# A score matrix product by seven products, split into two passes with a second level of seven

## The chip, the cores and the metric

The kernel runs on one core of one Trainium2 chip. The metric is the device time of one execution in microseconds. A core has a matrix engine (PE, with its weight loads shown apart as PEld), a vector engine (DVE), a scalar engine (ACT), a further elementwise engine (POOL) and a queue engine that here issues the DMAs (SP). Matrix products are summed in PSUM, which has eight banks of 128 x 512 fp32; everything else lies in SBUF or in DRAM.

## The reference, cut to what matters

One layer of a perceiver: cross-attention of 128 latents `x` to a context of 12544 rows, then a small linear attention and a feed-forward block on the 128 latents.

```
q = (layernorm(x) @ Wq) per head / sqrt(128)      # 16 heads, 128 queries
k = ctx @ Wk ; v = ctx @ Wv                       # ctx: 12544 x 512
attn = softmax(q k^T) ; x = x + (attn v) @ Wo
x = x + linear_attention(layernorm(x)) ; x = x + ffn(layernorm(x))
```

Nearly all the work lies in the first attention. The kernel folds `Wk` into the queries: `kq = Wk_h q_h^T` for all heads is a 512 x 2048 matrix (16 heads x 128 queries), so the scores are `ctx (12544 x 512) @ kq (512 x 2048)`. The weighted sums are then `ctx^T @ exp(scores)`, and `Wv`, `Wo` are applied to the small result.

## The kernel before

**Stages in order.** A prologue makes `kq` (lines L356 and L385). The scores stage (L196) makes all scores and stores them in DRAM (`sc`). The weighing stage (L490) reads them back, subtracts the column maximum, takes the exponential, and multiplies with the context. The rest of the layer works on 128 rows.

**fp32 as three products.** An operand is cut in a high part (a rounded copy, type fp32r, by ACT) and a low part (operand minus high part, by DVE). A product is three matrix products, low x high, high x low and high x high, summed in one PSUM bank.

**The scores stage.** The context has 49 row pairs `i` (two blocks of 128 rows), the columns of `kq` two halves `f` of 1024. A unit `(i, f)` is a 256 x 512 by 512 x 1024 product, done by the Strassen-Winograd scheme: seven products of 128 x 256 by 256 x 512 instead of eight. The context's sums are `S1..S4` (`sum_ct`, DVE, L169 to L172), the column sums `T1..T4` are made once. A product is two contraction chunks of three matmuls, so six matmuls; a unit is 42, and the stage 98 x 42 = 4116. Out of the products come four blocks of the scores:

```
p1 = A11 B11   p6 = S2 T2   p7 = S3 T3   p5 = S1 T1   p4 = A22 T4   p2 = A12 B21   p3 = S4 B22
u2 = p1 + p6   u3 = u2 + p7
c11 = p1 + p2   c22 = u3 + p5   c21 = u3 + p4   c12 = u2 + p5 + p3
```

DVE adds (L225) read one product from PSUM and one sum from SBUF; ACT copies `p1` and `c11` out (L231, L260); DVE keeps a running maximum (L243); one 1 MB store for each unit goes to DRAM (L235). PSUM holds eight banks in turn.

**What sets the order.** The steps stand on each engine in the order in which they are written (`seq`); in the prologue and the first four units this order is written out by hand as a list of names (`plan`), after that a scheduler of the framework places them. The pairs go `(i, 0), (i, 1)` for i from 2; at the end both last pairs of half 0 go before those of half 1, so that POOL can reduce the maximum of half 0 over the partitions (L592) while PE still works on half 1, and the first exponentials are ready when the scores end (`beside`).

**The weighing stage.** 98 steps of 128 rows for each half; a step is 24 matmuls (two column halves, four blocks of the context, three parts), with DVE and ACT preparing the exponentials two steps ahead (`soften`, `high_part`, `low_part`, `total`).

Of the kernel before, what the change touches and what calls it, by code (L numbers as in the profile page):

```python
# [16 lines left out]
P = 128  # L17
D = 512
# [15 lines left out]
def tile_perceiver_layer(  # L34
# [34 lines left out]
    x1 = const.tile([P, D], F32, name="x1")  # L69
# [62 lines left out]
    S1, S2, S3, S4, A11, A12, A22, A21 = range(8)  # L132
    B11, T2, T3, T1, T4, B21, B22 = range(7)
# [4 lines left out]
    ctp = att.enter_context(tc.tile_pool(name="ct", bufs=2))  # L138
    mxp = att.enter_context(tc.tile_pool(name="mx", bufs=1))
    p1x = ExitStack()  # L140
    tmp = p1x.enter_context(tc.tile_pool(name="tmp", bufs=1))
    kqx = ExitStack()
    kq1p = ctx.enter_context(tc.tile_pool(name="kq1", bufs=1, side="right"))
    kq0p = kqx.enter_context(tc.tile_pool(name="kq0", bufs=1, side="right"))
    kq = {}

    def right(f, s, n):

        if (f, s) not in kq:
            kq[f, s] = (kq0p, kq1p)[f].tile([P, 2, 2, 512], F32R, name=f"kq{f}_{s}")  # L150
        return kq[f, s][:, n, :, :]

    def spare(s, shape):

        return kq1p.tile(shape, F32, name=f"kq1_{s}")

    def load_ct(i):
        if i == 1:
            raw = spare(B22, [P, 8, 2, P])
        else:  # L160
            raw = ctp.tile([P, 8, 2, P], F32, tag="raw", name="ctr", bufs=1)
        nc.sync.dma_start(out=raw[:, A11:, :, :], in_=cT[i])
        return raw

    def sum_ct(raw):

        r = lambda s: raw[:, s, :, :]
        return [
            lambda: nc.vector.tensor_tensor(r(S1), r(A21), r(A22), ALU.add),  # L169
            lambda: nc.vector.tensor_tensor(r(S3), r(A11), r(A21), ALU.subtract),  # L170
            lambda: nc.vector.tensor_tensor(r(S2), r(S1), r(A11), ALU.subtract),
            lambda: seq(nc.vector.tensor_tensor(r(S4), r(A12), r(S2), ALU.subtract)),  # L172
        ]

    def high_ct(raw):
        hi = ctp.tile([P, 7, 2, P], F32R, tag="hi", name="cth")
        return hi, nc.scalar.copy(hi, raw[:, :7, :, :])  # L177

    def low_ct(raw, hi, lo=None):
        if lo is None:  # L180
            lo = ctp.tile([P, 7, 2, P], F32R, tag="lo", name="ctl")
        return lo, nc.vector.tensor_tensor(lo, raw[:, :7, :, :], hi, ALU.subtract)  # L182

    cts, raws, mx = {}, {}, {}

    def unit(i, f, place):

        t = {}

        def product(ps, a, b, first):  # L190
            n = 0
            hi, lo = cts[i]
            for cc in range(2):
                for lt, part in ((lo, 0), (hi, 1), (hi, 0)):
                    place(
                        nc.tensor.matmul(  # L196
                            ps, lhsT=lt[:, a, cc, :], rhs=right(f, b, part)[:, cc, :], start=(first and n == 0),
                            stop=(n == 5), skip_group_check=True,
                        )
                    )  # L200
                    n += 1

        def fresh(p, a, b):
            def emit():
                t[p] = ps_s.tile([P, 512], F32, tag="s", name="ps")
                product(t[p], a, b, True)

            return emit

        def onto(p, a, b):  # L210
            return lambda: product(t[p], a, b, False)

        def out(j, b):
            if "so" not in t:
                t["so"] = iop.tile([P, 2, 1024], F32, tag="io", name="so")
            return t["so"][:, j, b * 512 : (b + 1) * 512]

        def add(name, p, q):
            def emit():
                if name in ("u2", "u3"):  # L220
                    t[name] = tmp.tile([P, 512], F32, tag=name, name=name)
                    to = t[name]
                else:
                    to = out(*name)
                place(nc.vector.tensor_tensor(to, t[p], t[q], ALU.add))  # L225

            return emit

        def p1s():
            t["p1s"] = tmp.tile([P, 512], F32, tag="p1", name="p1s")  # L230
            place(nc.scalar.copy(t["p1s"], t["p1"]))  # L231

        def c12():
            add((0, 1), "p5", "u2")()
            nc.sync.dma_start(out=sc_d[i][f], in_=t["so"])  # L235

        def larger(j):
            def emit():
                if f not in mx:
                    mx[f] = mxp.tile([P, 1024], F32, name=f"mx{f}")  # L240
                    place(nc.vector.tensor_tensor(mx[f], t["so"][:, 1, :], t["so"][:, 0, :], ALU.max))
                elif i > 0:
                    place(nc.vector.tensor_tensor(mx[f], mx[f], t["so"][:, j, :], ALU.max))  # L243

            return emit

        return t, {
            "p1": fresh("p1", A11, B11),
            "p1s": p1s,
            "p6": fresh("p6", S2, T2),  # L250
            "U2": add("u2", "p6", "p1s"),
            "p7": fresh("p7", S3, T3),
# [11 lines left out]
        }  # L264

# [64 lines left out]
    for h2 in range(4, 8):  # L335
        ws.append(load_w(h2))
        begin(*ws[h2][2])
        if h2 == 4:
            raws[1] = load_ct(1)
# [1187 lines left out]
```

## Time and profile before

| | us |
|---|---|
| three timed runs | 2111.97, 2112.01, 2112.11; median 2112.01 |
| span of the profiled execution, first to last instruction | 2109.8 |
| median less the span (what lies around it) | 2.2 |

The profile gives the span of its execution; no other time of that execution is listed. It was taken on the one core at a granted PE clock of 1.000.

| part of the span | from, us | length, us |
|---|---|---|
| prologue, up to the first scores matmul | 0 | 35.55 |
| scores, 4116 matmuls | 35.55 | 933.19 |
| weighing, 4704 matmuls | 968.75 | 1066.24 |
| the rest of the layer | 2034.98 | 74.8 |

The busy columns of a page say how long an engine had an instruction running; the line after a bar in a group says how long the engine stood idle before these instructions and whom it waited for.

### The profile page before, as it was taken

What the parts mean: (1) busy time and instruction counts of PE and PEld (TensorE: products, weight loads), DVE (VectorE), ACT (ScalarE), POOL (GpSimd) and SP (SyncE); (2) the same over time, 40 slices, a digit from 0 to 9 for tenths busy, and PEclk for the clock granted to TensorE, in tenths of its full rate; (3) what the DMA queues carried; (4) which work ended last, traced back from release to release, by engine and by line L of the source; (5) the groups of instructions that cost most, each with busy time, mean ns of one, the idle gap of its engine ahead of it and who ended that gap; (6) DMA issues with size and microseconds to landing.
All of it is one profiled execution on the core that took longest, in us unless ns stands there. A gap on an engine that the chain in (4) does not pass through costs nothing.

```text
span 2109.8 us, 24119 instructions
## 1 busy us (share of the span) xinstructions
PE 2103.4 (100%) x9614; PEld 1742.1 (83%) x9614; DVE 1689.0 (80%) x1908; ACT 776.9 (37%) x898; POOL 55.6 (3%) x23
## 2 busy tenths in 40 slices
PE   9999999999999999999999999999999999999999
PEld 8888888888888888888888888888888888888896
DVE  6877777777777777778897888879898887777767
ACT  6222122221222122214444444445544455444445
POOL 0000000000000000000000000003020000000010
PEclk9999999999999999999999999999999999999999
DMA  6333333333333333336564455555545454434443
GB/s 216 142 137 138 132 150 130 141 129 150 130 150 128 142 143 137 140 150 229 200 237 152 172 207 199 200 199 185 184 155 195 157 202 161 141 143 145 150 156 126
DMA packets 73877, 341.74 MB, mean 162 GB/s; under 512 B 8451, under 2 KB 12803, under 8 KB 46499
## 3 DMA queue, kind: packets, MB, share of 16 engines
q1 hardware_dynamic: 73622, 340.09, 43.7%
q8 instruction: 75, 1.23, 0.2%
q14 instruction: 36, 0.29, 0.0%
q10 hardware_dynamic: 144, 0.13, 0.0%
HBM read 228.76 MB, written 111.43 MB: 161 GB/s over the span
## 4 chain that ended last, share of the span: by engine, by line
PE 99%; DVE 1%; ACT 0%; DMA 0%; issue 0%; DVEq 0%
PE pu L490 51%; PE ps L196 44%; PE pq L356 1%; PE pk L385 1%; PE pc L897 1%; PE po L932 1%; PE py L1438 0%; PE pv L1112 0%; DMA x<-in_x_dram 0%; DVE uT L1408 0%; PE pq L1112 0%; PE pk L1112 0%; PE pp L1249 0%; DVE am L1425 0%; DVE st L1381 0%; PE ph L1352 0%
## 5 line engine op out<-in xcount | busy, mean ns | idle before, releaser
L196 PE MATMUL ps<-kq,cth 128*128 128x512 f32 x2744 | 844.9, 389 | 0.0
L490 PE MATMUL pu<-ph,cl 128*128 128x512 f32 x1568 | 610.0, 389 | 0.0
L490 PE MATMUL pu<-pl,ch 128*128 128x512 f32 x1568 | 610.0, 389 | 0.0
L490 PE MATMUL pu<-ph,ch 128*128 128x512 f32 x1568 | 610.0, 389 | 0.0
L196 PEld LDWEIGHTS ps<-kq,cth 128*128 128x128 f32 x2744 | 515.0, 188 | 107.0
L196 PE MATMUL ps<-kq,ctl 128*128 128x512 f32 x1344 | 522.8, 389 | 0.0
L544 ACT CAST ph<-si 128x1024 fp32r<-128x1024 f32 x194 | 204.1, 1052 | 449.5 <-PE pu L490 449.1
L490 PEld LDWEIGHTS pu<-ph,ch 128*128 128x128 f32 x1568 | 294.3, 188 | 61.2
L490 PEld LDWEIGHTS pu<-ph,cl 128*128 128x128 f32 x1568 | 294.3, 188 | 61.1
L490 PEld LDWEIGHTS pu<-pl,ch 128*128 128x128 f32 x1568 | 294.3, 188 | 61.0
L225 DVE TENSOR_TENSOR so<-ps,u 128x512 f32<-128x512 f32 x294 | 202.6, 690 | 133.9 <-PE ps L196 129.5
L196 PEld LDWEIGHTS ps<-kq,ctl 128*128 128x128 f32 x1344 | 252.3, 188 | 52.3
L260 ACT COPY so<-ps 128x512 f32<-128x512 f32 x98 | 57.7, 589 | 577.4 <-PE ps L196 577.4
L532 DVE TENSOR_TENSOR cl<-cr,ch 128x1024 fp32r<-128x1024 f32 x98 | 126.2, 1288 | 167.5 <-ACT ch L526 167.5
L539 ACT ACTIVATE si<-si 128x1024 f32<-128x1024 f32 x194 | 205.5, 1059 | 96.6 <-DVE si L538 96.6
L549 DVE TENSOR_TENSOR pl<-si,ph 128x1024 fp32r<-128x1024 f32 x194 | 240.0, 1237 | 1.0 <-ACT ph L544 1.0
L243 DVE TENSOR_TENSOR mx<-mx,so 128x1024 f32<-128x1024 f32 x190 | 232.1, 1222 | 6.8
L538 DVE TENSOR_TENSOR si<-si,mb 128x1024 f32<-128x1024 f32 x194 | 235.4, 1214 | 0.0
L557 DVE TENSOR_TENSOR lsum<-lsum,si 128x1024 f32<-128x1024 f32 x192 | 233.7, 1217 | 0.0
L526 ACT CAST ch<-cr 128x1024 fp32r<-128x1024 f32 x98 | 102.4, 1045 | 0.1
L177 ACT CAST cth<-ctr 128x1792 fp32r<-128x1792 f32 x48 | 81.8, 1703 | 37.8 <-PE ps L196 35.4
L182 DVE TENSOR_TENSOR ctl<-ctr,cth 128x1792 fp32r<-128x1792 f32 x47 | 94.9, 2019 | 0.7 <-ACT cth L177 0.7
(291 smaller groups left out, 872.7 us busy)
## 6 DMA issues: line engine op xcount, KB each, us to landing
sc<-so SPq DMA_DIRECT2D x98, 1024.0 KB, 3.8
si<-sc SPq DMA_DIRECT2D x97, 1024.0 KB, 5.1
cr<-in_c_dram SPq DMA_DIRECT2D x98, 512.0 KB, 3.5
ctr<-in_cT_dram SPq DMA_DIRECT2D x48, 512.0 KB, 3.5
kq<-in_w1T_dram SPq DMA_DIRECT2D x16, 512.0 KB, 4.2
kq<-in_w2T_dram SPq DMA_DIRECT2D x16, 512.0 KB, 4.0
ternary<-kq SPq DMA_DIRECT2D x4, 1024.0 KB, 10.2
kq<-ternary SPq DMA_DIRECT2D x4, 1024.0 KB, 9.4
```

Of the source, the lines that this page charges most:

```text
L182: return lo, nc.vector.tensor_tensor(lo, raw[:, :7, :, :], hi, ALU.subtract)
L196: nc.tensor.matmul(ps, lhsT=lt[:, a, cc, :], rhs=right(f, b, part)[:, cc, :], start=(first and n == 0), stop=(n == 5), skip_group_check=True,)
L225: place(nc.vector.tensor_tensor(to, t[p], t[q], ALU.add))
L243: place(nc.vector.tensor_tensor(mx[f], mx[f], t["so"][:, j, :], ALU.max))
L490: nc.tensor.matmul(pu[b][cc], lhsT=lt[:, j, cs], rhs=rt[:, bs], start=(first and n == 0), stop=(last and n == 2))
L526: seq(nc.scalar.copy(ctx_hi[f, i], ctx_raw[f, i]))
L532: seq(nc.vector.tensor_tensor(ctx_lo[f, i], ctx_raw[f, i], ctx_hi[f, i], ALU.subtract))
L538: seq(nc.vector.tensor_tensor(exps[k], exps[k], mb[f], ALU.subtract))
L539: seq(nc.scalar.activation(exps[k], exps[k], AF.Exp))
L544: seq(nc.scalar.copy(high[k], exps[k]))
L549: seq(nc.vector.tensor_tensor(low[k], exps[k], high[k], ALU.subtract))
L557: seq(nc.vector.tensor_tensor(lsum[f], lsum[f], exps[k], ALU.add))
```

## The change

The scores stage is written anew; prologue, weighing stage and the rest keep their work.

**Groups and slots.** Two row pairs are taken together, times both halves: 24 groups of four units (`"00"`, `"01"`, `"10"`, `"11"`: pair, half), and pair 48 alone. A slot is the three matmuls of one contraction chunk of 128. A product of one unit is two slots, so four units need eight slots for it.

**A second level of seven.** For `p1`, `p6` and `p7` the four units of a group form again a 2 x 2 by 2 x 2 block product (pairs x chunks by chunks x halves). The function `wide` makes them with seven slots, from sums of the left blocks (`left_sums`, now on POOL) and of the `kq` blocks (`sums`, made once). The other four products stay eight slots (`direct`).

**Two passes.** The first pass goes over all groups with 22 slots each: `p1` (7), `p2` (8) and `p6` (7); it stores `c11` and, for later, `u2`. The second goes over all groups with 31 slots: `p7` (7), `p5`, `p3`, `p4` (8 each); it loads `u2` and stores `c22`, `c12`, `c21`. The `kq` operands of the second pass are put into DRAM early in the first (`put_by`) and brought back (`bring_back`).

**Seeded banks.** A sum that was an elementwise add is now made in PSUM: ACT copies the earlier sum from SBUF into a bank (`act(ps, ...)`), and the matmuls are added onto it (`start=False`). Inside `wide` the bank is read ("tapped") between two slots while later slots go on adding to it.

**Order.** All steps up to the first exponentials are given to a planner (`Plan`) with an engine, a length, what they read and write, and a due time. It walks through time, gives each engine that is free the ready step with the earliest due time, and the order that comes out is the program's. It counts for `n` elements 0.09 + 0.00097 n us on ACT, 0.157 + 0.00104 n on DVE, 0.2 + 0.0021 n on POOL, and 0.68 us a slot; it lets no POOL step run beside a DVE step marked `port` (both inputs in SBUF).

**Smaller parts.** Every score block has a store of its own (262 KB in place of 1 MB), the context's blocks are loaded in pieces of 262 KB, some of them twice. The last pair comes first in the first pass and last in the second; the maximum of half 0 is complete only with its `c21`. The first exponentials' loads and steps are given to the planner too.

Core of the diff (the new functions that the text speaks of; the removed ones are those named above):

```diff
+    W_LEFT = ("a00", "a01", "s2", "s3", "a11", "s1", "s4")
+    W_SLOTS = (("p1", 0), ("p6", 5), ("p2", 6), ("p7", 10), ("p5", 11), ("p4", 15), ("p3", 16))
+    def wide(R_, h, x, z, y, t0, dst, fold=None):
...
+        def tap(u, n):
+            if fold:
+                dve(dst[u], x, fold[u], ALU.add, after(n), port=False)
+            else:
+                act(dst[u], x, after(n))
+        slot(x, a["a00"], R_["b00"], True, due["p1"])
+        if fold:
+            dve(z, x, fold["00"], ALU.add, after("p1"), port=False)
+        else:
+            act(z, x, after("p1"))
+        slot(x, a["s2"], R_["t2"], False, due["p6"])
+        tap("01", "p6")
+        slot(z, a["a01"], R_["b10"], False, due["p2"])
+        act(dst["00"], z, after("p2"))
+        slot(x, a["s3"], R_["t3"], False, due["p7"])
+        tap("11", "p7")
+        slot(y, a["s1"], R_["t1"], True, due["p5"])
+        dve(dst["11"], y, dst["11"], ALU.add, after("p5"), port=False)
+        slot(x, a["a11"], R_["t4"], False, due["p4"])
+        tap("10", "p4")
+        slot(y, a["s4"], R_["b11"], False, due["p3"])
+        dve(dst["01"], y, dst["01"], ALU.add, after("p3"), port=False)
+    def left_sums(a, due):
+        s = lambda k: left_raw(a + k)
+        pool(s(2), s(0), s(1), ALU.add, due)
+        pool(s(6), s(2), s(4), ALU.subtract, due)
+        pool(s(7), s(4), s(0), ALU.subtract, due)
+        pool(s(3), s(5), s(6), ALU.subtract, due)
...
+    def first(g):
+        n, G = g % 2, TA + 22 * SLOT * g
+        wide(R[1], 0, bank(0), bank(2), bank(3), G, m1s)
+        for u, s0, s1 in D_FIRST:
...
+            act(ps, m1s[u], G + (s0 - 1.5) * SLOT)
+            direct(ps, D_HI[n], D_LO[n], R[2], r_, f, G + s0 * SLOT, G + s1 * SLOT, False)
+            act(c11, ps, G + (s1 + 1) * SLOT)
+            largest(ps, f, 0, G + (s1 + 1.5) * SLOT, True)
+            store(c11, pair_of(g, u), f, 0, 0, G + (s1 + 2) * SLOT)
+        u2 = dict(zip(UNIT, u2c))
+        wide(R[6], 14, bank(1), bank(2), bank(4), G + 14 * SLOT, u2, m1s)
...
+    def second(g):
+        G = TB + 31 * SLOT * g
...
+        u2 = {u: load_u2(g, u, G - 14 * SLOT) for u in at_slots}
+        wide(R[7], 0, bank(0), bank(2), bank(3), G, m7s)
+        for u, (a0, a1, b0, b1, c0_, c1) in at_slots.items():
...
+            act(ps, u2[u], t(a0 - 2))
+            direct(ps, *S1_, R[5], r_, f, t(a0), t(a1), False)
+            dve(c22, ps, m7s[u], ALU.add, t(a1 + 1), port=False)
+            pool(u2[u], u2[u], m7s[u], ALU.add, t(a1 + 1))
+            largest(c22, f, 1, t(a1 + 3), False)
+            store(c22, i, f, 1, 1, t(a1 + 3))
+            direct(ps, *S4_, R[3], r_, f, t(b0), t(b1), False)
+            act(c12, ps, t(b1 + 1))
+            largest(ps, f, 1, t(b1 + 1.5), True)
+            store(c12, i, f, 0, 1, t(b1 + 2))
...
+            act(ps4, u2[u], t(c0_ - 2))
+            direct(ps4, *A22_, R[4], r_, f, t(c0_), t(c1), False)
+            act(c21, ps4, t(c1 + 1))
+            largest(ps4, f, 0, t(c1 + 1.5), True)
+            store(c21, i, f, 1, 0, t(c1 + 2))
...
+    def bring_back(k, x, due, into=None):
+        n, to = waiting_of[k, x], into or through
+        dma(lambda: to.ap, lambda: waiting_d[:, n, :], 262 * MB_US, due, [("wait", n)], keys_of(to))
+        cut(*R[k][x], to, due + 5, 3)
...
+    plan.add("POOL", 3.3, bound, [("mx", 0, 0), ("mx", 0, 1)], [("mb",)] + kk("M"), E - 14, port=True)
...
+        plan.add("DVE", 1.22, lambda k=k: shifted(k), [("mb",)] + keys, keys, E - 9 + k, port=True)
+        plan.add("ACT", 1.06, lambda k=k: powered(k), keys, keys, E - 8 + k)
+        plan.add("ACT", 1.05, lambda k=k: high_part(k), keys, hk_, E - 6 + k)
+        plan.add("DVE", 1.24, lambda k=k: low_part(k), keys + hk_, lk_, E - 4 + k, port=True)
+    plan.run()
```

The single lines that cut a `left` block (`left_parts`: ACT high part, DVE low part) cut four or three blocks of 128 x 128 in one instruction.

## The prediction

> **What bounds the kernel now.** First the page's busy line and the chain that ended last, by engine; then the same chain in order of time.
>
> ```profile
> span 2109.8 us, 24119 instructions
> PE 2103.4 (100%) x9614; PEld 1742.1 (83%) x9614; DVE 1689.0 (80%) x1908; ACT 776.9 (37%) x898; POOL 55.6 (3%) x23
> PE 99%; DVE 1%; ACT 0%; DMA 0%; issue 0%; DVEq 0%
> ...
> 35.55 933.19 PE ps L196 x4116
> 968.75 1066.24 PE pu L490 x4704
> ```
>
> PE never waits between 35.55 and 2034.98. A scores matmul costs 933.19 / 4116 = 0.2267 us, a weighing matmul the same (1066.24 / 4704). A matmul taken away is worth 0.2267 us as long as PE still never waits. So the question is what the smaller matmul count makes the other engines do, and where PE waits for them for the first time. I read prices from the groups kept apart by form:
>
> ```profile
> L225 DVE TENSOR_TENSOR so<-ps,u 128x512 f32<-128x512 f32 x294 | 202.6, 690 | 133.9 <-PE ps L196 129.5
> L260 ACT COPY so<-ps 128x512 f32<-128x512 f32 x98 | 57.7, 589 | 577.4 <-PE ps L196 577.4
> L549 DVE TENSOR_TENSOR pl<-si,ph 128x1024 fp32r<-128x1024 f32 x194 | 240.0, 1237 | 1.0 <-ACT ph L544 1.0
> L986 POOL TENSOR_SCALAR_AFFINE_SELECT decay<-decay 128x2048 f32<-128x2048 f32 x1 | 2.0, 2018 | 11.6 <-ACT decay L985 11.6
> ```
>
> After the bar stand busy time and mean ns of one. A 128x512 step costs 0.69 us on DVE and 0.59 on ACT; POOL has no two-input elementwise row at all. The timelines of DVE and POOL show what happens when both want SBUF:
>
> ```profile
> 952.01 3.25 POOL L592 PARTITION_ALL_REDUCE mb<-mx  x1 [949.97 <-DVE mx L243]
> 952.53 0.69 DVE L225 TENSOR_TENSOR u<-ps,p1s 128x512 f32<-128x512 f32 x1 [0.77 <-PE ps L196]
> 953.82 0.69 DVE L225 TENSOR_TENSOR u<-ps,u 128x512 f32<-128x512 f32 x1 [0.60 <-PE ps L196]
> ...
> 1435.76 16.00 POOL L809 PARTITION_ALL_REDUCE sums<-sums  x1 [324.82 <-DVE sums L808]
> 1449.59 2.25 DVE L532 TENSOR_TENSOR cl<-cr,ch 128x1024 fp32r<-128x1024 f32 x1 [0.93 <-ACT ch L526]
> 1451.67 3.30 POOL L809 PARTITION_ALL_REDUCE mb<-mx  x1
> 1451.76 2.96 DVE L549 TENSOR_TENSOR pl<-si,ph 128x1024 fp32r<-128x1024 f32 x1
> ```
>
> A DVE add with one input in PSUM runs at 0.69 us inside a POOL reduce. A DVE step with both inputs in SBUF is stretched (2.25 and 2.96 us for a usual 1.22), and POOL's reduce takes 16.00 us for the 4.06 that its two later sisters take. So POOL and two-SBUF-input DVE steps exclude each other; below I count them on one shared "port".
>
> **Part 1, matmuls removed: -47.6 us.** A group of four units had 4 x 42 = 168 matmuls; now 22 + 31 = 53 slots of three, 159. 24 groups save 216. Pair 48 had 84 and gets 30 slots (12 + 4 + 12, and 2 because one sum of columns is not kept and is made of two products): 90. The changed program's PE order holds 3906 matmuls of this form, 210 fewer: 210 x 0.2267 = 47.6. All of it is on the path.
>
> **Part 2, ACT and DVE in a group: 0, hidden.** First pass, 22 slots = 14.96 us: DVE 8 adds, 4 maxima, 3 cuts of 512 and 2 of 384 (0.55, between the 256 and 512 rows) = 15 x 0.69 + 1.1 = 11.5; ACT 17 x 0.59 + 2 x 0.46 = 10.9. Second pass, 31 slots = 21.08 us: DVE 2 adds, 4 `c22`, 12 maxima, 4 + 1 cuts = 22 x 0.69 + 0.55 = 15.7; ACT 25 x 0.59 + 0.46 = 15.2. ACT's copies into PSUM have no row; the SBUF cast of 128x512 takes 0.61 and the copy out of PSUM 0.59, so I take 0.59. The cover is the slots placed between: in the order after, two slots on one `wide` bank stand five apart, so four slots, 2.7 us, cover one tap of 0.59 or 0.69, and a seeded bank has over eight slots between its last read and its next use. If this cover went, each `wide` would show its seven taps, some 0.6 us each.
>
> **Part 3, POOL and the port: 0, but the tightest place.** Each group gives POOL, first pass, 8 adds of 128x128 and 2 of 128x512; second, 4 of 128x128, 4 of 128x512 for the left blocks and 4 of 128x512 for `u3`. Call the price of 512 p and that of 128 q. Below: the one-input select, 0.29 for 128x128 and 2.02 for 128x2048, makes p 0.64 by a straight line. Above: the maximum reduce of 1024 in 3.25 us makes 1.62 for 512, the adding reduce of 6.11 us makes 3.06. I take the plan's own count, p = 1.27, q = 0.47, which lies between the two nearest of these. On the port in the second pass: DVE's cuts and `c22` maxima, 8 x 0.69 + 0.55 = 6.1, and POOL 8p + 4q: 6.3, 12.0, 14.6 or 27.5 for the four prices. Sums: 12.4, **18.1**, 20.7 or 33.6 of 21.08 us. At 18.1 the port is 86% full and I take no loss. In the first pass the sum is 3.2 + 6.3 = 9.5 of 14.96. A late POOL result delays the cuts for the next group, and these the next `wide`.
>
> The Trainium skill speaks against this part: "GPSIMD Engine Reference", section "Performance versus the Vector engine", puts a 2048-element fp32 add at 4497 ns, twice DVE, and advises DVE for elementwise work. No run here shows it; by a quarter of that figure p would be an estimated 1.12 and the port sum still fit.
>
> **Part 4, DMAs: 0.** SP issues 1139 DMAs for 436. First pass, 13 x 0.262 MB = 3.4 MB in 14.96 us, 228 GB/s (245 in the groups that also bring an operand back); second, 20 x 0.262 = 5.2 MB in 21.08, 249 GB/s. The windows show what queued transfers of 0.5 MB reach, and what the scores stage uses now:
>
> ```profile
> 20.00:30.00 10.00, 10.00 (x92) 9.98 (x90) 7.11 (x9) 8.62 (x15) 0.00 (x0) 1.00 1.08 372
> 200.00:400.00 200.00, 200.00 (x884) 165.62 (x883) 154.03 (x198) 42.25 (x53) 0.00 (x0) 1.00 0.34 137
> ```
>
> The last two columns are the DMA engines' busy share and GB/s. 249 is two thirds of 372, so transfers stay hidden. The queue itself can hurt: a store that waits for its block holds the loads behind it on SP, and a late left load ends as a late `wide`; the loads stand some 20 slots (13 us) ahead against a landing of 3 to 4 us.
>
> The skill's "SBUF — State Buffer", section on the setup-cost knee, gives 224 GB/s for 256 KiB transfers and wants larger ones. Taken as a limit it would make a group of the second pass 5.24 MB / 224 GB/s = 23.4 us and one of the first 15.2, an estimated 62 us in all, and the kernel some 30 us slower; the row of 372, with many transfers in flight, is why I don't take it so.
>
> **Part 5, the start: +5 us (0 to 12).** Before, the first unit needs only `B11`, and DVE makes the rest beside it. Now, before the first `wide`, the order after has 31 DVE steps of 512, 7 of 1024 and 3 of 256: 31 x 0.69 + 7 x 1.22 + 3 x 0.42 = 31.2 us, or 27.6 at the spacing of back-to-back rows (0.60, 1.135, 0.34). They can't begin before 15.3 (first cut of `kq` in the trace: 15.75, for the larger tile), so the first `wide` starts at 43 to 46.5; PE has slots up to 35.55 + 13 x 0.68 = 44.4. Then the first group has few other slots to put between the taps: four uncovered taps of about 0.6. Sum 2.4 to 4.5, and something for cuts that come late: 5.
>
> **Part 6, the change of passes: +4 us (0 to 9).** `kq` operands for `p4` come back through one room that also holds one of `p7`'s taps: a load (2.84 us for 256 KB, the load of `x`) + 0.61 + 0.69 = 4.1 for each; three in a row are 12.4, against 21 slots = 14.3 us before the first `p4`. If the room is late by a round or two, 4.1 to 8.2 show. I take one.
>
> **Part 7, the end of the scores: +6.7 us (5 to 9).** Before, POOL reduced half 0 at 952.01, 17 us ahead of the end. Now half 0's maximum is complete only with the `c21` of pair 48, and PE has four slots (2.7 us) left behind it. Then nothing covers ACT copy 0.59 + DVE maximum 0.69 + POOL reduce 3.25 + DVE shift 1.22 + ACT exponential 1.06 + ACT high part 1.05 + DVE low part 1.24 (the second matmul needs it) = 9.1; less 2.7 - and less the one matmul that may go before - 6.2, and 0.5 for seven hand-overs of 0.02 to 0.1.
>
> **Sum.** -47.6 + 5 + 4 + 6.7 = -31.9; I add 2 for small waits in 48 groups, the first of which the plan's order can't know. Span 2109.8 - 29.9 = 2079.9; the 2.2 us that median and span differ by are kept: **2082**. A difference under 0.2% (4.2 us) counts as none here.
>
> **Rivals.**
> *All waits hidden* (0.10): parts 5 and 6 cost nothing, part 7 5 us: 2112 - 47.6 + 5 = 2069. For it: ACT and DVE have a quarter idle. Against it: part 5 is DVE's full queue (9.76 of 10 us busy at 30 to 40 even before).
> *The second pass limps* (0.16): blocked DVE steps delay taps by 0.5 to 1.3 us a group, 12 to 31 us: 2094 to 2113. For it: every blocked DVE step also holds the taps queued behind it.
> *The port becomes the bound, slower* (0.16): a POOL add of 512 costs 1.62 or more, and a tenth of the port is lost between holders: 20.7 / 0.9 = 22.9 us a group, 1.9 too many, 24 x 1.9 = 45: 2127. It decides from 29.9 / 24 = 1.25 us a group, a port sum of 0.9 x 22.3 = 20.1, so p about 1.55; at 3.06 it would be hundreds.
> *The matmuls are not fewer*: excluded by the counted order.
>
> **Numbers.** Likeliest 2082 (0.58; 2072 to 2093 by itself). The range 2067 to 2118 takes in the first two rivals and the mild part of the third, and leaves out some 0.15, most of it above. Faster by over 0.2%: 0.58 + 0.10 + 0.11 of the limping case = 0.79; same: its other 0.05; slower: 0.16.
>
> **What would show it.** Right: 3906 matmuls, PE's gaps at three places only (43 to 65 us, the change of passes near 410, the end of the scores near 935), no PE wait inside the steady groups, POOL's 128x512 rows near 1.2 us. Wrong: regular PE waits on `bank` tiles for DVE in the second pass with POOL over 90% or DVE steps stretched beside it; or loads of `craw` that land late behind waiting stores.

## The result, and the profile after

Before: 2111.99 us, median of 4 runs (2111.57 to 2112.11). After: 2133.37 us, median of 4 (2129.96 to 2135.60). The ratio is 1.0101, 95% interval 1.0086 to 1.0115: **1% slower**, where I forecast 1.4% faster. The profiled execution of the kernel after took 2129.96 us, the fastest of its four, and its span is 2128.3; the four runs scatter by 5.6 us, those of the kernel before by 0.5.

The busy line and the chain that ended last, by engine and line:

```profile
span 2128.3 us, 27212 instructions
...
PE 2086.8 (98%) x9402; PEld 1702.4 (80%) x9406; DVE 1666.2 (78%) x1994; ACT 1185.3 (56%) x1778; POOL 531.0 (25%) x557
...
PE 79%; DMA 7%; DVE 4%; ACT 2%; issue 2%; POOL 1%; SPq 0%; ACTq 0%; DVEq 0%; POOLq 0%
```

PE was 99% of the chain and is now 79%: DMA, DVE, ACT and POOL have come into it. The windows show where (after the length, busy time and instructions of PE, PEld, DVE, ACT, POOL; then granted clock, DMA share, GB/s):

```profile
36.00:75.00 39.00, 31.97 (x115) 23.35 (x114) 29.88 (x40) 21.22 (x39) 13.32 (x16) 0.87 0.75 257
75.00:140.00 65.00, 60.18 (x255) 48.22 (x254) 46.56 (x73) 41.51 (x78) 27.89 (x43) 0.97 0.72 228
140.00:395.00 255.00, 252.27 (x1107) 206.66 (x1106) 187.55 (x292) 178.33 (x326) 107.64 (x164) 1.00 0.72 231
395.00:450.00 55.00, 50.84 (x218) 40.25 (x217) 41.33 (x58) 36.29 (x67) 28.66 (x34) 1.00 0.80 264
450.00:955.00 505.00, 495.09 (x2122) 393.87 (x2122) 382.77 (x529) 319.25 (x596) 296.74 (x272) 1.00 0.73 235
```

Count instructions here, not busy time (the busy time of PE hides small waits: in the pages a matmul is busy for 0.39 us, and the next starts 0.227 us after it): a stretch in which PE never waits holds its length / 0.2267 matmuls. The kernel before has 2230 between 450 and 955; this one has 2122, so 505 - 2122 x 0.2267 = 23.9 us are lost, in many small waits. No engine is full there: DVE 76%, ACT 63%, POOL 59%, DMA 73%.

Below, "PE lost" is the distance from each scores matmul's start to the next, less 0.2267, summed over a range of matmuls by number, so that all kernels are compared over the same work. "Change" is the first group of the second pass, "second pass" its next 22 groups. "End" is PE's wait before the weighing, and what the weighing takes beyond the 1066 us of before.

| kernel | start, 1-96 | first pass, -1614 | change, -1707 | second pass, -3753 | end | time, us |
|---|---|---|---|---|---|---|
| before (4116 matmuls) | 0.3 | 0 | 0 | 0 | 0 | 2112.0 |
| after (3906) | 13.5 | 13.3 | 5.4 | 23.7 | 5.8 + 3.2 | 2133.4 |
| u3_narrow | 13.0 | 8.1 | 5.3 | 9.8 | 5.8 + 2.6 | 2113.6 |
| max_narrow | 13.2 | 11.0 | 9.0 | 11.0 | 5.8 + 2.3 | 2118.2 |
| no_loads | 13.5 | 13.5 | 5.3 | 10.4 | 5.8 + 3.1 | 2117.1 |
| stores_by_act | 14.2 | 11.2 | 5.6 | 11.2 | 6.8 + 2.1 | 2117.5 |
| u3_by_dve | 11.8 | 14.5 | 6.0 | 28.1 | 5.7 + 3.4 | 2136.0 |
| pool_price | 13.6 | 13.8 | 8.0 | 32.3 | 5.7 + 3.2 | 2134.8 |
| dma_price | 13.2 | 47.5 | 6.0 | 29.2 | 5.7 + 3.4 | 2169.3 |
| both_prices | 14.3 | 15.6 | 6.8 | 44.0 | 5.8 + 2.0 | 2154.4 |
| spaced | 11.9 | 8.3 | 7.9 | 66.2 | 5.7 + 2.8 | 2172.9 |
| spaced_u3_narrow | 15.6 | 11.8 | 5.2 | 5.2 | 5.7 + 3.5 | 2112.0 |
| warm | 14.2 | 10.1 | 7.9 | 23.3 | 5.8 + 0.9 | 2129.1 |
| start_narrow | 10.0 | 11.6 | 8.1 | 24.9 | 5.8 + 2.1 | 2132.5 |
| early_end | 13.1 | 13.2 | 7.4 | 21.4 | 0 + 1.6 | 2123.4 |
| act_end | 13.2 | 11.8 | 7.7 | 10.9 | 0 + 6.5 | 2117.0 |
| act_all | 13.3 | 21.5 | 6.0 | 10.7 | 0 + 6.4 | 2123.4 |
| act_end_spaced | 13.4 | 13.7 | 6.6 | 49.6 | 0.1 + 5.7 | 2155.3 |
| queue_and_end | 13.2 | 12.5 | 6.6 | 11.8 | 0 + 1.6 | 2110.9 |
| copy_known | 13.2 | 13.4 | 7.5 | 11.1 | 0 + 1.4 | 2111.7 |

Times are medians, the losses come from one profile each. A profiled run can lie up to 8 us from its kernel's median (pool_price: 2142.9 for 2134.8). Between profiles of kernels with the same steps in the same order up to there, the start differs from 11.8 to 15.6 us (u3_by_dve, spaced_u3_narrow) and the first pass from 8.1 to 14.5 (u3_narrow, u3_by_dve); only differences beyond that are read below. The row after, with 1.0 us after matmul 3753, is the whole difference of the two profiles: 13.5 + 13.3 + 5.4 + 23.7 + 1.0 + 9.0 - 47.6 = 18.3 of 2128.3 - 2109.8 = 18.5.

### The profile page after: what moved, and what is told of

Same layout as the page of the kernel before. It is cut to its first block, busy times and chain, and to the rows that moved or that the text cites. A ratio compares the mean times of both kernels' runs of the same rounds, so it can differ in the third digit from the quotient of the medians.

```text
span 2128.3 us, 27212 instructions
## 1 busy us (share of the span) xinstructions
PE 2086.8 (98%) x9402; PEld 1702.4 (80%) x9406; DVE 1666.2 (78%) x1994; ACT 1185.3 (56%) x1778; POOL 531.0 (25%) x557
## 4 chain that ended last, share of the span: by engine, by line
PE 79%; DMA 7%; DVE 4%; ACT 2%; issue 2%; POOL 1%; SPq 0%; ACTq 0%; DVEq 0%; POOLq 0%
PE pu L956 50%; PE bank L333 26%; DMA sc<-uT 3%; DMA io<-u 1%; DVE mx L630 1%; DMA sc<-io 1%; DMA craw<-in_cT_dram 1%; DVE uT L309 1%; POOL craw L319 1%; PE pc L1393 1%; DVE ccut L309 1%; PE po L1428 1%; ACT uT L305 0%; ACT ccut L305 0%; POOL io L319 0%
## 5 line engine op out<-in xcount | busy, mean ns | idle before, releaser
L333 PE MATMUL bank<-kq,ccut 128*128 128x512 f32 x1548 | 385.5, 394 | 11.9 <-DVE uT L309 9.5
L333 PEld LDWEIGHTS bank<-kq,ccut 128*128 128x128 f32 x1548 | 286.1, 188 | 91.4 <-DVE uT L309 29.3
L630 DVE TENSOR_TENSOR mx<-mx,bank 128x512 f32<-128x512 f32 x288 | 197.0, 684 | 148.6 <-ACT uT L305 70.1
L333 PE MATMUL bank<-uT,ccut 128*128 128x512 f32 x1104 | 286.4, 393 | 8.6 <-ACT io L305 4.0
L319 POOL TENSOR_TENSOR craw<-craw 128x128 f32<-128x128 f32 (+2 forms) x339 | 220.6, 668 | 152.9 <-DMA craw<-in_cT_dram 109.9
L333 PEld LDWEIGHTS bank<-uT,ccut 128*128 128x128 f32 x1104 | 208.0, 189 | 56.0 <-ACT io L305 5.3
L305 ACT COPY io<-bank 128x512 f32<-128x512 f32 x318 | 184.1, 588 | 76.4 <-PE bank L333 28.9
L309 DVE TENSOR_TENSOR ccut<-craw,ccut 128x512 fp32r<-128x512 f32 (+2 forms) x247 | 175.0, 722 | 50.3 <-ACT ccut L305 43.7
L305 ACT COPY bank<-io 128x512 f32<-128x512 f32 x290 | 171.8, 593 | 46.1 <-DVE mx L630 31.2
L305 ACT COPY uT<-bank 128x512 f32<-128x512 f32 x194 | 113.5, 586 | 145.9 <-PE bank L333 90.6
```

The lines of the kernel that those rows point to most:

```text
L305: plan.add("ACT", 0.09 + 0.00097 * src.elements, lambda: seq(nc.scalar.copy(dst.ap, src.ap)), keys_of(src), keys_of(dst), due)
L309: "DVE", 0.157 + 0.00104 * dst.elements, lambda: seq(nc.vector.tensor_tensor(dst.ap, a.ap, b.ap, op)),
L319: "POOL", 0.2 + 0.0021 * dst.elements, lambda: seq(nc.gpsimd.tensor_tensor(dst.ap, a.ap, b.ap, op)),
L333: nc.tensor.matmul(ps.ap, lhsT=a.ap, rhs=b.ap, start=(start and n == 0), stop=(n == 2), skip_group_check=True)
L630: seq(nc.vector.tensor_tensor(mx[f][:, cs], mx[f][:, cs], room.ap, ALU.max))
```

## How a wait reaches PE in the second pass

What PE waits for, its weight loads first (sum, times, longest), then what ACT and DVE wait for there:

```profile
PEld bank L333 <- DVE uT L309: 28.1, 48, 1.5
...
PE bank L333 <- DVE uT L309: 9.4, 18, 1.1
...
ACT uT L305 <- DMA sc<-uT: 30.4, 24, 2.2
...
DVE mx L630 <- ACT uT L305: 68.5, 77, 2.0
```

PE waits for hardly anything but DVE's `c22` add (`uT<-bank,io`): it reads the bank on which the `s4` products are then added. By matmul number, 14.4 of the 23.7 us lie ahead of the first `s4` slot of unit `"00"` of each group, 5.0 ahead of that of `"11"` and 1.3 ahead of that of `"01"`. The add is late because of what stands ahead of it in DVE's order. One such place in the timeline (start, length; in brackets the idle time before it and what ended it):

```profile
615.15 0.59 ACT L305 COPY uT<-bank 128x512 f32<-128x512 f32 x1 [1.07 <-DMA sc<-uT]
615.63 0.62 ACT L305 CAST ccut<-craw 128x512 fp32r<-128x512 f32 x1
...
616.28 0.69 DVE L309 TENSOR_TENSOR ccut<-craw,ccut 128x512 fp32r<-128x512 f32 x1 [1.75 <-DMA sc<-uT]
...
616.89 0.68 DVE L309 TENSOR_TENSOR uT<-bank,io 128x512 f32<-128x512 f32 x1
...
617.63 3.27 PEld L333 LDWEIGHTS bank<-kq,ccut 128*128 128x128 f32 x15 [0.85 <-DVE uT L309]
```

ACT copies a result into its room (one of a few buffers in SBUF that the blocks take in turn) only when the last store from that room has landed; ACT's cut stands behind that copy, DVE's cut behind ACT's (it starts at 616.28, as ACT's ends at 616.25; its bracket names the store), the `c22` add behind DVE's cut, and PE behind the add.

A wait that I had not looked for is the 68.5 us: DVE's maximum over a bank waits for ACT's copy of the same bank. The Trainium skill has a reason in "PSUM — Partial Sum Buffer", section "PSUM bank collisions raise a hardware error": two engines must not access one bank at once, reads included. The row shows the two reads one after the other; what two at once would do, no run shows. That this wait holds PE is not shown either: in u3_narrow and max_narrow below it is longer (80.1 and 113.3 us), while PE loses less than half.

POOL's adds of 512 take 1.33 and 1.47 us for the plan's 1.27, and DVE's maximum with both inputs in SBUF takes 1.10 us on average, for 0.69 where no POOL step runs (at 617.61):

```profile
L319 POOL TENSOR_TENSOR io<-io 128x512 f32<-128x512 f32 x92 | 122.1, 1327 | 117.4 <-ACT io L305 117.0 <-ACT bank L305 0.4
L319 POOL TENSOR_TENSOR craw<-craw 128x512 f32<-128x512 f32 x44 | 64.7, 1470 | 85.9 <-DMA craw<-in_cT_dram 54.7 <-DVE mx L630 29.7
...
L630 DVE TENSOR_TENSOR mx<-mx,uT 128x512 f32<-128x512 f32 x92 | 101.5, 1103 | 2.3
...
L630 DVE TENSOR_TENSOR mx<-mx,bank 128x512 f32<-128x512 f32 x183 | 125.0, 683 | 77.2 <-ACT uT L305 68.5 <-PE bank L333 7.5
```

The first pass, for comparison, loses most in its third to fifth groups: 7.7 of its 13.3 us (matmuls 162 to 360), and 6.2 to 9.5 in the kernels whose first pass has the same order. The longest of these waits, in the timeline:

```profile
126.75 1.81 POOL L319 TENSOR_TENSOR craw<-craw 128x128 f32<-128x128 f32 x4 [6.97 <-DMA craw<-in_cT_dram]
127.27 0.62 ACT L305 CAST kq<-io 128x512 fp32r<-128x512 f32 x1 [4.36 <-DMA io<-waiting]
127.80 0.51 ACT L305 CAST ccut<-craw 128x384 fp32r<-128x384 f32 x1
128.21 1.06 ACT L305 COPY io<-bank 128x512 f32<-128x512 f32 x2
...
129.33 0.96 PE L333 MATMUL bank<-uT,ccut 128*128 128x512 f32 x2 [2.22 <-ACT io L305]
```

A block of the context and an operand that is brought back land late; ACT's casts wait for them (the second through POOL's add), and ACT's copy out of a bank, for which PE waits, stands behind the casts. No experiment takes this apart; the rest of the first pass's loss comes and goes between profiles (0.6 us in u3_narrow, 6.7 in early_end).

So for the second pass there were two theories: **P**, POOL and the port it shares with DVE; **D**, the transfers (rooms, landing, and SP's one queue).

## The experiments

**1. Less POOL, less DVE, fewer transfers, one at a time.** In u3_narrow the add of `u3`, in max_narrow the maximum over `c22` cover 64 columns; no_loads leaves out the second pass's loads from its third group on.

```diff
-            pool(u2[u], u2[u], m7s[u], ALU.add, t(a1 + 1))
+            plan.add(
+                "POOL", 0.2 + 0.0021 * 512,
+                lambda u2_=u2[u], m7_=m7s[u]: seq(nc.gpsimd.tensor_tensor(u2_.ap[:, :64], u2_.ap[:, :64], m7_.ap[:, :64], ALU.add)),
...
-            largest(c22, f, 1, t(a1 + 3), False)
+            largest(c22, f, 1, t(a1 + 3), False, 64)
...
-        plan.add("SP", size_, lambda: nc.sync.dma_start(out=dst(), in_=src()), reads, writes, due)
+        emit = (lambda: None) if left_out else (lambda: nc.sync.dma_start(out=dst(), in_=src()))
+        plan.add("SP", size_, emit, reads, writes, due)
```

u3_narrow: 

> POOL's add that makes u3 in the second pass covers 64 of its 512 columns (the other 448 of u3 are left at u2); every instruction keeps its place in the order. The second pass loses 24.3 us of PE time between 450 and 955 us of the profile after. Theory P (POOL's adds, 1.33 to 1.47 us where the plan counts 1.27, make the second pass late): each of the 92 steady adds gets some 0.9 us shorter, the loss falls below 6 us, the kernel to 2106-2114 us. Theory D (transfers: stores and loads of 256 KB land 4.6 us after their issue, where the plan counts 2.9, and hold ACT, DVE and the loads behind them): POOL is not the cause, the loss stays above 18 us, 2127-2134 us. Theory C (the clock at half speed after a long PE wait, and the start): nothing in the second pass changes, 2130 us.

max_narrow: 

> DVE's maximum over c22, the step with both inputs in SBUF that takes 1.08 us beside POOL for 0.69, covers 64 of its 512 columns in the second pass; POOL's work and the order are left as they are. The page after has PE wait for DVE's c22 add, not for POOL. Theory PE-DVE (DVE is blocked by POOL in this maximum and comes late to the next c22 add, on which the bank's next products wait): the loss of the second pass falls from 23.8 us to under 10, as it did with POOL's u3 add shortened, the kernel to 2108-2116 us. Theory PE-POOL (POOL's own results come late, as it is too slow): the loss stays above 18, 2125-2133 us.

no_loads: 

> The second pass leaves out its loads from its third group on (the blocks of the left operand and u2: 8 of 20 transfers of a group, 40% of its bytes; it works on what the rooms held); order and all steps of PE, ACT, DVE and POOL stay. Theory D (transfers hold the second pass): the loss of 23.8 us falls below 10, 2110-2118 us. Theory P (POOL and DVE exclude each other): it stays at 16 us or more, 2124-2133 us. The losses before 440 us (some 32 us) stay under both.

Measured: 2113.6 us (ratio to before 1.0003, 0.9993 to 1.0012), 2118.2 (1.0031, 1.0019 to 1.0043) and 2117.1 (1.0030, 1.0018 to 1.0041). P's direction was right on two of them and D's on the third, though the losses left (9.8, 11.0 and 10.4 us) lie above the bounds given (6, 10 and 10): each alone takes 13 to 14 of the 23.7 us, and each leaves about the same remainder. The wait list says why. "ACT uT <- DMA sc<-uT", 30.4 us after, is 1.1 in u3_narrow, 2.2 in max_narrow and absent in no_loads, and PE's waits come down to nearly the same row in all three (in this order):

```profile
PEld bank L333 <- DVE uT L309: 15.4, 45, 0.4
```

```profile
PEld bank L333 <- DVE uT L309: 15.7, 45, 0.7
```

```profile
PEld bank L334 <- DVE uT L309: 15.5, 45, 0.6
```

That three unlike cuts remove the same waits and the same 13 us speaks for one loop, of which the two theories are ends: late DVE steps make PE late, late results make late stores, late stores keep rooms, and kept rooms delay ACT and with it DVE. Not every kind of slack does: in experiments 3 and 5 POOL and ACT, or the `c22` add, get more room, and the second pass loses more.

**2. A better price in the plan.** Only the order changes.

```diff
-            "POOL", 0.2 + 0.0021 * dst.elements,
+            "POOL", 0.26 + 0.0024 * dst.elements,     # pool_price, both_prices
-                        end = lines + 1.8
+                        end = lines + 3.2                  # dma_price, both_prices
```

pool_price: 

> Only the plan's price of a POOL add is raised, to what the profile after shows (0.57 us for 128x128, 1.49 for 128x512, for 0.47 and 1.27); the same instructions, in another order. Theory P in the form that the order is what is wrong (POOL has room, but is planned too tight): the second pass loses 5 to 10 us for 24.3, the kernel takes 2110-2120 us. Theory P in the form that the port is simply full (POOL 13.3 us and DVE's two-SBUF steps 6 us of 21.1): no order helps, 2128 us or more. Theory D: no change beyond 5 us, 2126-2136 us; the first pass's losses (7.6 us from 75 to 140, 4.6 from 140 to 395) stay under every theory.

dma_price: 

> Only the plan's time from a transfer's end on the line to its landing is raised, 1.8 to 3.2 us, which makes a 256 KB transfer land 4.3 us after its issue for the measured 4.6; the same instructions in another order. Theory D: the losses of the first pass (7.6 us from 75 to 140, 4.6 from 140 to 395) go to 2 us or less, and most of the second pass's 24.3 us too: 2100-2112 us. Theory P: the first pass gains its 10 us, but the second pass stays at 24 us or gets worse, as its order is still made for a POOL add of 1.27: 2118-2140 us.

both_prices: 

> The plan's prices of POOL adds and of landing are both raised as in the two other kernels. Theories P and D together (a planned order that is made with wrong prices): the first pass's 12 us between 75 and 395 go to 1, the second pass's 24.3 to some 10: 2104-2114 us. If the port is full whatever the order: 2122-2130 us. What stays under all of them are the start (13.8 us from 0 to 75, half of it in stretches at half clock), the change of passes (5) and the end of the scores (7).

Measured: 2134.8 (1.0103, 1.0086 to 1.0120), 2169.3 (1.0270, 1.0255 to 1.0285), 2154.4 (1.0200, 1.0185 to 1.0215). None came out faster. pool_price lies where "the port is full" and theory D had put it; the other two are slower than every expectation. An order made with prices nearer to the trace is no better, and with the longer landing it loses 47.5 us in the first pass, for 13.3. So these two prices are not what was wrong by themselves; why the new orders lose more is not shown.

**3. POOL's sum moved to DVE.** One DVE add of `u2` and `m7` writes `u3` into the bank; POOL's add and ACT's copy go.

```diff
-            pool(u2[u], u2[u], m7s[u], ALU.add, t(a1 + 1))
-            act(ps4, u2[u], t(c0_ - 2))
+            dve(ps4, u2[u], m7s[u], ALU.add, t(c0_ - 2.5))
```

> The sum u3 is no longer made by POOL in place and then copied to its bank by ACT: one DVE add of u2 and m7 writes it into the bank. A group has 4 POOL adds of 512 (1.33 us each) and 4 ACT copies (0.59) less, and 4 DVE adds more (0.69 to 0.9). Everything is computed. Theory P: POOL falls to 8 us of a group of 21.1, the port sum with the DVE steps stays near 17; the loss of the second pass falls from 23.8 to 8-14 us, 2113-2122 us. If DVE's own queue is the limit (15.7 + 2.8 to 3.6 us of 21.1): no gain, 2128-2140 us.

2136.0 (1.0120, 1.0103 to 1.0137): no gain; the second pass loses 28.1. POOL fell to 177 of 505 us, DVE rose to 422, and DVE itself now waits 24.1 us for stores. PE still waits for the `c22` add, but at another place: 18.1 of the 28.1 us lie ahead of the first `s4` slot of `"01"`, next to none at that of `"00"`. So POOL's time was not the limit by itself; that it is DVE's order which counts fits this, and is argued, not shown.

**4. The queue.** The stores of `c12` and `c21` leave SP; ACT issues each one copy after the copy that it stores. SP's step stays in the plan and issues nothing.

```diff
+        def emit():
+            seq(nc.scalar.copy(dst.ap, src.ap))
+            for send in sends:
+                seq(send())
+            sends[:] = send_after.pop(n, ())
...
-            store(c12, i, f, 0, 1, t(b1 + 2))
+            store(c12, i, f, 0, 1, t(b1 + 2), n12)
```

> In the second pass the stores of c12 and c21 are issued from ACT's own queue, one copy after the copy that they store, and no longer from SP, where they stand in one order with the loads; bytes, rooms and all steps stay. Theory Q (no_loads helped since SP's queue stands still: loads wait behind stores whose copy isn't made yet; SP waited 317 of 505 us): 23.8 falls to 10-15 us, 2116-2124 us. Theory B (it helped since there were 40% less bytes, so that stores landed sooner): no gain, 2128-2140 us, more if the issue of eight stores a group costs ACT time.

2117.5 (1.0028, 1.0015 to 1.0040), everything computed, as theory Q had it. As many bytes, rooms and steps as after; what changed is who issues 192 of the stores, and when. First the issues of the kernel after and SP's two longest waits in its second pass, then the issues and ACT's waits of this one:

```profile
sc<-uT SPq DMA_DIRECT2D x294, 256.0 KB, 4.6
...
SPq L324 <- POOL craw L319: 111.0, 22, 5.9
SPq L324 <- ACT uT L305: 93.8, 84, 3.0
```

```profile
sc<-uT ACTq DMA_DIRECT2D x192, 256.0 KB, 3.8
sc<-uT SPq DMA_DIRECT2D x102, 256.0 KB, 4.3
...
ACT uT L310 <- DMA sc<-uT: 1.2, 1, 1.2
```

The stores landed 4.6 us after their issue and now 3.8, and the 30.4 us of waiting for rooms are 1.2. On SP a store that waits for its copy (93.8 us) also holds the loads behind it, and a load that waits for its room (111.0) holds the stores. So of theory D the one queue is enough to account for the gain, with the bytes as they were. It does not spread: with the first pass's stores of `c11` on ACT as well (act_all, below) the first pass lost 21.5 us.

**5. The spacing.** The 45 waits that remain in u3_narrow lie at the first two of the places named above, before the first `s4` slot of `"00"` and of `"11"`, where three and two slots (2.04 and 1.36 us) cover the `c22` add. (`"10"` has two as well and shows no such wait.) In the diff, a unit's six numbers are its two slots on `s1`, on `s4` and on `a22`.

```diff
-    D_SECOND = {"00": (7, 8, 12, 13, 21, 22), "11": (9, 14, 17, 18, 27, 28), "10": (19, 20, 23, 24, 32, 33), "01": (25, 26, 29, 30, 34, 35)}
+    D_SECOND = {"00": (7, 8, 13, 14, 21, 22), "11": (9, 12, 19, 20, 27, 28), "10": (17, 18, 23, 24, 29, 30), "01": (25, 26, 32, 33, 34, 35)}
```

spaced: 

> Only the slots of the second pass are placed anew: between a unit's second slot on s1 (after which DVE must read the bank for c22) and its first slot on s4 (which adds on to the bank) there are four slots or more for each unit, where three of four units had two (1.36 us, for a DVE add of 0.69 that may find another step ahead of it). Theory S (some 10 us of the second pass's 23.8 are those places: in the three kernels in which POOL's add, DVE's maximum or the loads were cut, 45 waits of 0.35 us for that add stayed): 23.8 falls to 11-15, 2118-2124 us. Rival (the pass is held as a whole, a wait taken away at one place comes back at another): 20 or more, 2127-2136 us.

spaced_u3_narrow: 

> Both: the slots placed anew and POOL's u3 add cut to 64 of 512 columns (u3 is left wrong in the rest). Theory S: the two parts of the loss are separate and both go, under 3 us of 23.8 are left, 2098-2107 us. Rival: the 10 us that u3_narrow kept are something else than the spacing, 2108-2116 us.

2172.9 (1.0291, 1.0269 to 1.0312) and 2112.0 (0.9997, 0.9983 to 1.0011). With POOL's add cut, the second pass does fall from 9.8 to 5.2, where under 3 was expected, but the time is the rival's: the 1.6 us to u3_narrow are within the scatter of both. By itself the spacing costs 42 us, more than either expectation: PE's waits for the add are gone, and others stand in their place:

```profile
PEld bank L333 <- ACT bank L305: 52.4, 20, 3.7
...
ACT uT L305 <- DMA sc<-uT: 76.4, 22, 4.9
```

The seeds that ACT writes into the banks now come late, behind copies that wait for rooms.

**6. The start and the clock.** warm puts matmuls of zeros into three of PE's waits; start_narrow cuts POOL's two 512-wide adds of the first group to 16 columns of each 128.

```diff
+            slots, fill = 0, {8: (4, 18), 13: (4, 9), 1302: (3, 24)}   # after this slot: bank, matmuls
...
+            few = (lambda x: x[..., :16]) if dst.elements == 512 and TA - 5 * SLOT < due < TA else (lambda x: x)
```

warm: 

> PE is kept busy with matmuls of zeros into a free bank in three of its waits: 18 in the wait of 4.4 us at 41 us, 9 in that of 2.5 us at 52, 24 in that of 6 us at the end of the scores. Nothing else changes. Theory C (a wait of over 2 us lets the clock fall to half for 3.4 us or twice that): 11 + 8 matmuls in the start and some 11 in the weighing no longer take 0.427 us for 0.227, the granted clock is 1.00 there, and the kernel takes 5 to 7 us less, 2124-2129 us. Rival (those matmuls are slow since their operands come late, or the waits come from elsewhere): no change, 2130-2136 us.

start_narrow: 

> The changed kernel with POOL's two 512-wide adds of the first group's left operand (34.8 to 38.8 us) cut to an eighth of their columns, the order kept (the operand of the first group is left wrong). DVE's three adds of 1024 beside them took 5.94 us for 3.66 alone. Port theory for the start: these come to 4.5 us or less, PE's loss in the first 96 matmuls falls from 13.5 to 11-12 us, the kernel to 2131 us. Rival (ACT's cuts and the loads set the start): 13 us or more stay.

warm: 2129.1 (1.0080, 1.0065 to 1.0095), 4 us less, of which the profiles place 2.3: the weighing's extra falls from 3.2 to 0.9 us. The start stays (14.2), though the clock granted from 36 to 60 us rises from 0.79 to 0.94; that the faster matmuls there only wait longer for the same operands fits this. start_narrow: 2132.5 (1.0094, 1.0081 to 1.0107), within the scatter of the kernel after; its start loses 10.0 us, 1.8 below the least of the others. DVE's three adds of 1024, after and in start_narrow:

```profile
35.34 5.94 DVE L309 TENSOR_TENSOR kq<-kq,kq 128x1024 f32<-128x1024 f32 x3
```

```profile
35.25 4.01 DVE L309 TENSOR_TENSOR kq<-kq,kq 128x1024 f32<-128x1024 f32 x3
```

1.9 us of DVE's chain before the first group were POOL's presence; I had counted DVE's steps there and left POOL out. What the rest of the start's 13.5 is, no run separates.

**7. The end.** The last unit's cuts and outputs get cells and rooms of their own (they waited for those of the units before), and three DVE steps another due time.

```diff
+    LAST_CUTS = {8: (2, 9), 12: (4, 11), 16: (38, 40)}
...
-            c22, c12, c21 = (turn_of(k, outs_[k]) for k in ("c22", "c12", "c21"))
+            c22, c12, c21 = oc[:3]
```

> The last group's small unit gets cells and rooms of its own for its cuts and its three outputs (it waited for the cells and rooms of the units before it), and three DVE steps of the end another due time; so half 0's maximum is complete some 8 us earlier. Part 7 of the prediction: PE's wait before the weighing falls from 6.0 to some 2 us, and the clock no longer falls to half in the weighing (2.3 us): 2125-2129 us. Rival (another late step takes the place): 2130-2135 us.

2123.4 (1.0053, 1.0038 to 1.0068), better than expected. POOL's reduce of half 0 starts at 967.70 for 976.93, and PE's wait before the weighing, 5.8 us, is gone, with the half clock behind it: 5.8 + 1.6 = 7.4 us, which is the whole difference of the two spans (2128.3 and 2120.9). The medians differ by 10 since the profiled run after was the fastest of its four.

**8. Together.**

act_end: 

> Stores of c12 and c21 issued by ACT (as in stores_by_act) and the end with cells and rooms of its own (as in early_end); everything is computed. If the two are separate: 2133 - 16 - 10 = 2107 us, 2104-2110, with 11 us left in the second pass and under 2 us before the weighing. Rival (the end's gain came from a second pass that ran late, or the other way round): 2111-2117 us.

act_all: 

> As act_end, and the first pass's stores of c11 are issued by ACT too. Theory Q for the first pass as well: its losses from the second group on (7.7 us over matmuls 162 to 360, 5.3 over 360 to 1548) fall to some 5 in all, 2098-2105 us. Rival (there the rooms or the operands that are brought back hold it, not the order of the queue): no gain over act_end within 3 us, 2105-2110.

act_end_spaced: 

> As act_end, with the second pass's slots placed as in spaced. Theory S: with the queue relieved the 10 us that stay in the second pass (45 waits for DVE's c22 add) go as well: 2096-2102 us. Rival (spaced was slow since ACT's seeds wait in other places, 96 us of PE's waits there, and still do): slower than act_end, 2112-2145 us.

queue_and_end (as act_end, but in the last group SP issues the stores): 

> As act_end, but in the last group the stores of c12 and c21 are issued by SP as before. Everything is computed. If the weighing's extra 4.8 us (1072.7 for 1067.9) came from that store: 2117 - 5 = 2112 us, 2109-2114, level with the kernel before. If it came from something else: 2115-2119 us.

copy_known (`largest` also reads the room of ACT's copy, for the plan alone): 

> As queue_and_end, with one more thing told to the plan: that a maximum over a bank waits for ACT's copy of that bank. No step and no wait of the program changes, only the order. Theory R (DVE's order is made without that wait; idle time before mx<-mx,bank is 77 us in the second pass, nearly all for ACT uT): the 10 us that stay in the second pass fall to 5 or less, and something in the first pass too: 2100-2108 us. Rival (the order is not what matters, or the new order loses elsewhere as the other re-planned ones did): 2110-2130 us.

act_end: 2117.0 (1.0027, 1.0017 to 1.0037), no better than stores_by_act, as its rival had it. Its wait before the weighing is gone, but the weighing takes 6.5 us more, for one line:

```profile
973.50 0.69 DVE L320 TENSOR_TENSOR uT<-bank,uT 128x512 f32<-128x512 f32 x1 [4.97 <-DMA sc<-uT]
```

The store was issued only behind ACT's next copy, of which there was none for a while, and landed late; DVE's low part stood behind that add. With SP's stores in the last group, queue_and_end takes 2110.9 us (0.9995, 0.9986 to 1.0004): **level with the kernel before, 1.05% better than after**, the best version found. act_all: 2123.4 (1.0060, 1.0048 to 1.0072) and act_end_spaced: 2155.3 (1.0206, 1.0193 to 1.0219), both slower than any range stated for them. copy_known: 2111.7 (1.0002, 0.9991 to 1.0013), no gain, as its rival had it: that the plan didn't know of the maxima's wait is not what keeps the last 11 us.

## Why the prediction was wrong

- **Part 1** held: 3906 matmuls, 210 fewer, 47.6 us.
- **Part 2**, hidden ACT and DVE, is the step that failed. Its busy sums were right (DVE 382.77 / 505 of 21.08 is 16.0 us; I had 15.7), but a sum that fits is not cover: each step has a place in its engine's order. The cover that I counted was that of the taps, and of a seeded bank between its last read and its next use. I left out the read in between, DVE's `c22` add, for which the first `s4` slot waits: it has two or three slots, 1.36 to 2.04 us, not eight, and it stands behind cuts and copies, of which one can wait for the store from its room, a wait that was not on my list. PE's waits in the second pass are for this add. The second pass lost 23.7 us and the first 13.3, where "2 for small waits" stood. The second pass alone was the limping rival's 12 to 31, by the `c22` add and not by its taps; that rival had no first pass in it. The sign that I had named for being wrong came: regular PE waits on `bank` tiles for DVE, with DVE's maximum stretched beside POOL.
- **Part 3**: p measured 1.33 for the `u3` adds and 1.47 for the left operand's, for the 1.27 I took and within the bounds. That sharing the port costs nothing was wrong: DVE's maximum is stretched by 0.4 us, and POOL's adds are longer too. But the stretch alone is not the bound: in stores_by_act the maximum (1.07 us) and POOL's adds (1.32 and 1.49) are as long, and the second pass loses 11.2.
- **Part 4**: bytes were no limit (235 GB/s). The sentence on the queue had the right cause and dismissed it; the 13 us of lead were for loads, while the price was paid by stores and their rooms. stores_by_act puts 12.5 us on it in the second pass, the same 13 or so that the other three cuts remove, so these do not add up. A late left load, which the same sentence names, is one of the two loads behind the first pass's longest wait.
- **Part 5**: 13.5 for 5, beyond its bound of 12; 1.9 of it are DVE's adds stretched beside POOL. Less half clock there (warm) took nothing off it.
- **Part 6**: 5.4 for 4. **Part 7**: 9.0 for 6.7; the wait itself was 5.8, and of the other 3.2, in the weighing, the half clock is 1.6 to 2.3 (early_end, warm). Both were in range, and part 7 could be removed, as early_end shows.

By terms: start +8.5, first pass +13.3, second +23.7, change +1.4, end +2.3, rest +1.0, less the 2 I had added: 48.2; the median stands 5.1 us above the profiled span for my 2.2, since that run was the fastest of its four. That makes the 51 us between 2082 and 2133. Experiments account for some 13 of the second pass's 23.7 and 7.4 of the end's 9; the first pass's 13 and most of the start's are only located.

What stays open: the 10 to 12 us that are left in the second pass in every relieved kernel (spacing takes half of it, and only where POOL was relieved too), the first pass's 13, and why orders planned with other prices are worse. Taking the wait of a maximum on a copy away wasn't tried; both read one bank.

## What to carry to other kernels

Fewer matmuls are worth their time only while PE never waits; count matmuls in a stretch against its length, not busy time. Where an order is fixed in advance, ask of each step which rooms, banks and queue places it shares with steps of other engines: three quarters full everywhere was no slack here. A queue of its own for half of the stores was worth 16 us, and a shorter POOL add, a shorter maximum or fewer loads about as much; moving POOL's sum to DVE, spacing the slots and re-planning with other prices were worth nothing. Ask too what covers each read of a bank on which later products are added. Rooms of its own for the last unit took 7 us off the end.

## What the runs showed of the hardware that I had not expected

After some waits PE ran at half clock: the next 8 to 11 matmuls start 0.427 us apart for 0.227. In the kernel after it happened after waits of 4.4, 2.5, 2.4 and 5.8 us, and not after one of 1.9. The window after the longest (the granted clock is 0.66):

```profile
980.00:990.00 10.00, 5.88 (x13) 4.34 (x14) 7.68 (x7) 6.60 (x7) 0.17 (x1) 0.66 0.82 289
```

The Trainium skill, "TensorE: Matmul & The Clock Gate", section "What's actually happening", puts the half rate after an idle window of about 3.4 us; here shorter waits were enough in some places. The wait's length alone does not decide it: the half clock came after 1.9 us in early_end (at 52 us) and 2.0 in stores_by_act (at 94), and not after 2.9 in max_narrow (at 128) or 3.5 in u3_by_dve (at 446); after each wait of 3.7 us or more it came. Where PE had its operands it cost some 2 us (the weighing, in warm), in the start nothing that shows.
